# A second level of Strassen's algorithm in the second feed-forward matrix of an fp32 decoder block

## The chip, the cores and the metric

The kernel runs on one core of one Trainium2 chip. The metric is the device time of one execution in microseconds, from a median over several runs. Everything is computed in fp32.

## The reference

The input x has 4 batches of 2048 positions and 512 features. Three residual steps follow one another:

```
x = x + ssm(layernorm(x))              # linear recurrence over the 4 batches, features in groups of 64
x = x + cross_attention(layernorm(x))  # 16 heads of 32, 77 context rows for each batch
x = x + ffn(layernorm(x))

ffn: h = butterfly(x @ W_exp + b_exp, up_weights)      # 512 -> 2048, 11 butterfly stages
     h = gelu(h + up_bias)
     h = butterfly(h, down_weights)
     y = h @ W_con + b_con + down_bias                 # 2048 -> 512
```

The butterflies are linear, so the kernel multiplies them into the matrices beside them once: the feed-forward step becomes a 512 x 2048 matrix, a gelu, and a 2048 x 512 matrix. This case is about the second of the two.

## The kernel before

**Units.** The 2048 positions are cut into 16 units of 128. A unit has 4 x 128 rows (one tile of 128 for each batch), held as xt[P, 4, 512] with positions on the partitions. Each unit goes through `front` (recurrence, attention, the last layer norm and the sums `tb` that the first feed-forward matrix needs) and through `feed_forward`. The feed-forward of unit u and the front of unit u + 1 are woven together: `front` is a generator, and `step()` in `feed_forward` asks it for one more piece after every third step. A step is one product of the up half, or one of eight pieces of a product of the down half. A unit has 56 steps up and 56 down, and `front` has 33 pieces, so the front of the next unit ends before the unit does.

**Order on the engines.** The framework's scheduler orders each engine's instructions before the run, by the order of the code as priority and by its own estimate of when operands are ready; it adds all semaphores. An instruction whose operands are late in that estimate lets others go ahead, so matmuls of the two streams are mixed finely. SP issues all transfers, in one queue.

**One level of Strassen.** Both matrices use the seven-product form (Winograd's variant). For the second matrix (`down`, L606 to L643) the activations are four blocks a11, a12, a21, a22 of 1024 hidden rows by 256 positions, and the weights are seven combinations of 1024 x 256, made once in preparation and kept in DRAM as dn7 (L330 to L342). For each product `down` loads 1024 KB of weights into a buffer of the pool `wts` (three buffers, shared with the first matrix's w_up), and runs 8 x 2 matmuls: stationary an activation tile of 128 x 128, moving 256 columns of weights, summed over the eight hidden blocks in a PSUM bank:

```python
for p in range(h):
    for t in range(2):
        nc.tensor.matmul(ps[:, t, :], lhsT=act[p][lhs[i]][:, t, :], rhs=w[:, p, :], ...)
    step()
```

The products run in the order 5, 1, 6, 2, 7, 4, 3. Product 5 reads s1 = a21 + a22, which GpSimd makes for each hidden block in `up_tail` (L589). Between products GpSimd turns s1 into the other combinations (L621, L628), and VectorE adds the banks into xt, which is stored in four pieces.

**Attention, in `front`.** The query weights wq stay in SBUF for the whole run. For each batch tile: scores (L463), softmax on VectorE and ScalarE, scaling on GpSimd (L473), 16 transposes in four groups (L483) whose results pt are copied out of PSUM by VectorE and ScalarE in turn (L486, L488), the product with the values (L494) copied by VectorE into ot (L497), and the output projection (L501).

**Preparation.** `_prepare` builds both matrices before the first unit. The pieces of front(0) are woven in between. Its SBUF space (wup, wdn and smaller tiles) is given to the pools of the main loop (xlast, wts, ffn) afterwards, so these wait until its last stores have read it.

## Time and profile before

| | |
|---|---|
| median of 3 runs | 2728.4 us (2727.88 to 2728.4) |
| the profiled execution's own time | 2727.85 us |
| its span, first to last instruction | 2726.1 us |
| TensorE clock granted, mean | 0.990 |
| HBM read / written | 278.47 MB / 40.12 MB |
| w_dn loads | 112 of 1024 KB, 4.8 us to landing |
| w_up loads | 128 of 896 KB, 4.6 us to landing |

How to read it: PE is TensorE's matmuls, PEld its weight loads, which overlap the matmuls; DVE is VectorE, ACT ScalarE, POOL GpSimd, SP the engine that issues transfers. A group line gives line, engine, operation, output and inputs by the program's names, shapes and count, then busy us and the mean ns of one, then the engine's idle time just before and what ended it. An fp32 matmul stands in the profile as two records, each with its own weight load; a transpose is one record. [...]the rate is read from the starts of neighbours. The chain of waits is followed back from the last instruction to what released it each time.

### The profile page before, as it was taken

What the parts mean: (1) busy time and instruction counts of PE and PEld (TensorE: products, weight loads), DVE (VectorE), ACT (ScalarE), POOL (GpSimd) and SP (SyncE); (2) the same over time, 40 slices, a digit from 0 to 9 for tenths busy, and PEclk for the clock granted to TensorE, in tenths of its full rate; (3) what the DMA queues carried; (4) which work ended last, traced back from release to release, by engine and by line L of the source; (5) the groups of instructions that cost most, each with busy time, mean ns of one, the idle gap of its engine ahead of it and who ended that gap; (6) DMA issues with size and microseconds to landing.
All of it is one profiled execution on the core that took longest, in us unless ns stands there. A gap on an engine that the chain in (4) does not pass through costs nothing.

```text
span 2726.1 us, 34675 instructions
## 1 busy us (share of the span) xinstructions
PE 2626.3 (96%) x13448; PEld 2013.5 (74%) x13448; DVE 1308.1 (48%) x3148; ACT 794.3 (29%) x1456; POOL 778.7 (29%) x918
## 2 busy tenths in 40 slices
PE   6887999999999999999999999999999999999999
PEld 4545777786877778687777868777786877778688
DVE  4375544545454454545445454544545454454531
ACT  0222414223241422324142232414223241422321
POOL 4233231413223141322314132231413223141323
PEclk9888999999999999999999999999999999999999
DMA  7664233242423324242332424233232423323244
GB/s 234 213 246 173 89 111 110 78 135 78 143 89 112 111 76 135 78 143 89 113 109 77 135 78 143 89 114 109 76 136 78 143 89 111 112 77 120 78 141 137
DMA packets 96724, 320.84 MB, mean 118 GB/s; under 512 B 17584, under 2 KB 44336, under 8 KB 80432
## 3 DMA queue, kind: packets, MB, share of 16 engines
q1 hardware_dynamic: 96560, 318.62, 34.5%
q8 instruction: 107, 1.75, 0.2%
q14 instruction: 57, 0.47, 0.0%
HBM read 278.47 MB, written 40.12 MB: 117 GB/s over the span
## 4 chain that ended last, share of the span: by engine, by line
PE 83%; DVE 10%; POOL 4%; DMA 1%; issue 1%; ACT 0%; SPq 0%; POOLq 0%; DVEq 0%; ACTq 0%
PE ps_a L611 10%; PE ps_b L546 10%; PE ps_w L501 8%; PE ps_q L452 8%; PE ps_b L611 7%; PE ps_c L546 7%; PE ps_a L546 6%; PE ps_c L611 5%; PE ps_sc L463 5%; PE ps_pt L483 4%; PE ps_s L440 3%; POOL pr L473 2%; PE ps_t L399 2%; PE ps_o L494 2%; DVE st L377 2%
## 5 line engine op out<-in xcount | busy, mean ns | idle before, releaser
L589 POOL TENSOR_TENSOR s<-a,a 128x256 f32<-128x256 f32 x128 | 92.9, 726 | 1120.1 <-ACT a L551 1120.1
L546 PE MATMUL ps_b<-tb,w_up 128*128 128x256 f32 x1536 | 397.0, 379 | 0.7 <-DVE tb L518 0.7
L611 PE MATMUL ps_a<-w_dn,a 128*128 128x256 f32 x1536 | 372.1, 381 | 0.0
L611 PEld LDWEIGHTS ps_a<-w_dn,a 128*128 128x128 f32 x1536 | 282.3, 190 | 57.4 <-issue 20.3
L546 PEld LDWEIGHTS ps_b<-tb,w_up 128*128 128x128 f32 x1536 | 285.9, 190 | 51.1 <-issue 14.5
L551 ACT ACTIVATE a<-a,hbias 128x256 f32<-128x256 f32 x384 | 192.3, 508 | 270.4 <-DVE a L584 206.9
L546 PE MATMUL ps_a<-xnt,w_up 128*128 128x256 f32 x1024 | 269.0, 380 | 0.0
L611 PE MATMUL ps_c<-w_dn,s 128*128 128x256 f32 x1024 | 235.4, 381 | 7.3 <-POOL s L589 7.3
L501 PE MATMUL ps_w<-wo,ot 128*128 128x512 f32 x512 | 236.2, 604 | 4.8 <-DVE ot L497 4.8
L452 PE MATMUL ps_q<-xnt,wq 128*128 128x512 f32 x512 | 231.9, 596 | 0.7 <-ACT xnt L400 0.7
L611 PEld LDWEIGHTS ps_c<-w_dn,s 128*128 128x128 f32 x1024 | 191.0, 190 | 36.8 <-POOL s L589 11.4
L546 PEld LDWEIGHTS ps_a<-xnt,w_up 128*128 128x128 f32 x1024 | 190.4, 191 | 31.2 <-issue 7.2
L473 POOL TENSOR_TENSOR pr<-pr,sm 128x1232 f32<-128x1232 f32 x64 | 146.1, 2282 | 173.1 <-DVE sm L472 162.9
L501 PEld LDWEIGHTS ps_w<-wo,ot 128*128 128x128 f32 x512 | 96.3, 193 | 107.1 <-issue 94.4
L452 PEld LDWEIGHTS ps_q<-xnt,wq 128*128 128x128 f32 x512 | 97.9, 192 | 98.1 <-issue 93.9
L400 ACT COPY xnt<-ps_t 128x512 f32<-128x512 f32 x128 | 72.2, 588 | 331.4 <-PE ps_t L399 331.2
L469 ACT ACTIVATE pr<-pr 128x308 f32<-128x308 f32 x256 | 107.0, 455 | 206.7 <-DVE pr L468 206.2
L463 PE MATMUL ps_sc<-kbd,qt 128*128 128x308 f32 x512 | 163.3, 430 | 3.3 <-DVE pr L468 3.0
L483 PE MATMUL ps_pt<-ident,pr 128*77 128x128 f32 x1024 | 145.4, 281 | 19.2 <-POOL pr L473 13.6
L483 PEld LDWEIGHTS ps_pt<-ident,pr 128*77 128x77 f32 x1024 | 119.3, 150 | 56.5 <-POOL pr L473 19.7
L502 DVE TENSOR_TENSOR xt<-ps_w,xt 128x512 f32<-128x512 f32 x64 | 44.3, 692 | 235.0 <-PE ps_w L501 235.0
L599 POOL TENSOR_TENSOR xt<-xt,ybias 128x256 f32<-128x256 f32 x128 | 100.2, 818 | 184.4 <-DVE xn L396 184.4
(173 smaller groups left out, 3936.4 us busy)
## 6 DMA issues: line engine op xcount, KB each, us to landing
w_up<-up SPq DMA_DIRECT2D x128, 896.0 KB, 4.6
w_dn<-dn SPq DMA_DIRECT2D x112, 1024.0 KB, 4.8
xt<-in_x SPq DMA_DIRECT2D x16, 1024.0 KB, 5.5
out<-xt SPq DMA_DIRECT2D x64, 256.0 KB, 4.9
wdn<-in_wexp_t SPq DMA_DIRECT2D x4, 1024.0 KB, 10.9
rows_up<-wdn SPq DMA_DIRECT2D x16, 256.0 KB, 2.1
wdn<-rows_up SPq DMA_DIRECT2D x4, 1024.0 KB, 9.0
wdn<-in_wcon SPq DMA_DIRECT2D x4, 1024.0 KB, 4.8
```

The lines of the kernel that those rows point to most:

```text
L440: nc.tensor.matmul(ps[:, 2 * i : T, f * NS : (f + 1) * NS], lhsT=xpt[:, i, c * (P // NS) + f, :], rhs=gt[:, 0 : T - 2 * i, :], start=i == ...
L452: nc.tensor.matmul(ps, lhsT=wq[:, c, g * P : (g + 1) * P], rhs=xnt[:, c, :, :], start=c == 0, stop=c == NC - 1)
L463: nc.tensor.matmul(ps[:, 0 : 4 * NK], lhsT=qt[:, g, t, :], rhs=kbd[:, t, g, :], start=True, stop=True)
L469: nc.scalar.activation(pg, pg, AF.Exp, scale=1.0 / math.sqrt(DH))
L473: nc.gpsimd.tensor_tensor(pr, pr, sm.unsqueeze(2).to_broadcast([P, NH, NK]), ALU.mult)
L483: nc.tensor.transpose(pt_ps[0:NK, j, :], pr[:, 4 * g + j, :], ident)
L501: nc.tensor.matmul(ps, lhsT=ot[:, g, :], rhs=wo[:, g, :], start=g == 0, stop=g == NC - 1)
L546: nc.tensor.matmul(ps, lhsT=w[:, c, :], rhs=rhs[i - 1][:, c], start=first and c == 0, stop=c == 1, skip_group_check=True)
L551: nc.scalar.activation(out, x, AF.Gelu, bias=hbias[:, b : b + 1])
L589: nc.gpsimd.tensor_tensor(s1, a21, a22, ALU.add)
L599: nc.gpsimd.tensor_tensor(r, r, ybias[:, d], ALU.add)
L611: nc.tensor.matmul(ps[:, t, :], lhsT=act[p][lhs[i]][:, t, :], rhs=w[:, p, :], start=first and p == 0 and t == 0, stop=p == h - 1, skip_gro ...
```

## The change

The second matrix gets a second level: each of the seven products is itself done with seven products of 512 x 128 weights (49 in all).

- **Weights.** `_prepare` writes dn7[i] as seven 512 x 128 blocks: three copied as they are, four formed from the block by two VectorE and two GpSimd instructions in a double buffer. A product's weights are 1.75 MB and come in two loads of 1024 and 768 KB.
- **Activations.** The blocks a11 ... s1 become one tile each with eight hidden blocks, so that `operands` can form four combinations of four hidden blocks (512 columns) at a time, two on GpSimd and two on VectorE.
- **Matmuls.** 7 x 4 matmuls for each first-level product, with 128 moving columns; the seven results lie in two PSUM banks (tags a and b).
- **Folding.** One ScalarE copy and four VectorE sums take the seven results out of PSUM into pi, which is then added to the quarters of xt by VectorE or GpSimd.
- **Steps.** One step for each second-level product: 49 in the down half instead of 56. The order of first-level products becomes a11, s1, a12, s1 (changed), a22, s3, s1 (changed again). xt is stored in three pieces.
- **Attention.** wq no longer stays in SBUF; each unit loads it into the buffer of pt, which is now one tile for all four groups. All four pt copies and the ot copy are made by ScalarE.

```diff
@@ -27,6 +27,7 @@
 LOW = 7
 HIGH = 4
 LN_EPS = 1e-5
+DOWN = (0, 4, 1, 5, 3, 6, 2)
 MAGIC = 12582912.0
 
 
@@ -330,16 +331,23 @@
     h = NB // 2
     b11, b12, b21, b22 = (wdn[:, r * h : r * h + h, c * (D // 2) : (c + 1) * (D // 2)] for r in range(2) for c in range(2))
     t1, t2, t3, n4 = (wup[:, i, :].rearrange("p (b d) -> p b d", b=h) for i in range(4))
-    for i, w in ((0, b11), (1, b21), (2, b22)):
-        nc.sync.dma_start(out=dn7[i], in_=w)
     nc.vector.tensor_tensor(t1, b12, b11, ALU.subtract)
-    nc.sync.dma_start(out=dn7[4], in_=t1)
     nc.gpsimd.tensor_tensor(t3, b22, b12, ALU.subtract)
-    nc.sync.dma_start(out=dn7[6], in_=t3)
     nc.vector.tensor_tensor(t2, b22, t1, ALU.subtract)
-    nc.sync.dma_start(out=dn7[5], in_=t2)
     nc.vector.tensor_tensor(n4, b21, t2, ALU.subtract)
-    nc.sync.dma_start(out=dn7[3], in_=n4)
+    yield
+    st = pool.tile([P, 2, 4, h // 2, P], F32, tag="lowc", name="st")
+    y = (b11, b21, b22, n4, t1, t2, t3)
+    for n, i in enumerate(DOWN):
+        y11, y12, y21, y22 = (y[i][:, r * (h // 2) : (r + 1) * (h // 2), c * P : (c + 1) * P] for r in range(2) for c in range(2))
+        for k, w in ((0, y11), (1, y21), (6, y22)):
+            nc.sync.dma_start(out=dn7[i][:, k], in_=w)
+        s = st[:, n % 2]
+        nc.vector.tensor_tensor(s[:, 1], y12, y11, ALU.subtract)
+        nc.gpsimd.tensor_tensor(s[:, 3], y22, y12, ALU.subtract)
+        nc.vector.tensor_tensor(s[:, 2], y22, s[:, 1], ALU.subtract)
+        nc.gpsimd.tensor_tensor(s[:, 0], y21, s[:, 2], ALU.subtract)
+        nc.sync.dma_start(out=dn7[i][:, 2:6], in_=s)
     yield
 
 
@@ -358,7 +366,6 @@
     gt = const.tile([P, T, NS], F32, name="gt")
     kbd = const.tile([P, T, NC, 4 * NK], F32, name="kbd")
     vsb = const.tile([NK, T, D], F32, name="vsb")
-    wq = const.tile([P, NC, D], F32, name="wq")
     wo = const.tile([P, NC, D], F32, name="wo")
     hbias = const.tile([P, NB], F32, name="hbias")
     ybias = const.tile([P, D], F32, name="ybias")
@@ -443,6 +450,8 @@
             nc.vector.tensor_tensor(xc, ps, xc, ALU.add)
             yield
 
+        wq = work.tile([P, NC, D], F32, tag="pt", bufs=1, name="wq")
+        nc.sync.dma_start(out=wq, in_=wq_t.rearrange("(c p) e -> p c e", p=P))
         yield from normed(xt, got)
         xnt = got.pop()
         qt = work.tile([P, NC, T, P], F32, tag="qt", bufs=1, name="qt")
@@ -476,25 +485,20 @@
             if t == 0:
                 continue
             pr, tt = probs[t - 1], t - 1
-            pts = []
+            pt = work.tile([P, NC, 4, P], F32, tag="pt", bufs=1, name="pt")
             for g in range(NC):
                 pt_ps = psum.tile([P, 4, P], F32, tag="f", name="ps_pt")
                 for j in range(4):
                     nc.tensor.transpose(pt_ps[0:NK, j, :], pr[:, 4 * g + j, :], ident)
-                pt = work.tile([NK, 4, P], F32, tag="pt", bufs=4, name="pt")
-                if g % 2:
-                    nc.scalar.copy(pt, pt_ps[0:NK])
-                else:
-                    nc.vector.tensor_copy(pt, pt_ps[0:NK])
-                pts.append(pt)
+                nc.scalar.copy(pt[0:NK, g], pt_ps[0:NK])
             po = psum.tile([P, NC, P], F32, tag="f", name="ps_o")
             for g in range(NC):
                 for j in range(4):
                     h = 4 * g + j
                     nc.tensor.matmul(po[j * DH : (j + 1) * DH, g, :], lhsT=vsb[:, tt, h * DH : (h + 1) * DH],
-                                     rhs=pts[g][:, j, :], start=True, stop=True, tile_position=(0, j * DH))
+                                     rhs=pt[0:NK, g, j, :], start=True, stop=True, tile_position=(0, j * DH))
             ot = work.tile([P, NC, P], F32, tag="ot", bufs=1, name="ot")
-            nc.vector.tensor_copy(ot, po)
+            nc.scalar.copy(ot, po)
             yield
             ps = psum.tile([P, D], F32, tag="f", name="ps_w")
             for g in range(NC):
@@ -537,7 +542,7 @@
             return psum.tile([P, 512], F32, tag=tag, name=f"ps_{tag}")
 
         h = NB // 2
-        act = []
+        act = [ffn.tile([P, h, 2, P], F32, tag=g, bufs=1, name=g) for g in ("a11", "a12", "a21", "a22", "s1")]
         live = {}
 
         def up(p, i, ps, first):
@@ -567,19 +572,17 @@
         def up_mid(p):
             w, a, b, c, p1, u2 = live[p]
             up(p, 2, a, False)
-            a11, a12, a21, a22, s1 = (ffn.tile([P, 2, P], F32, tag=g, bufs=h, name=g)
-                                      for g in ("a11", "a12", "a21", "a22", "s1"))
+            a11, a12, a21, a22, s1 = (r[:, p] for r in act)
             gelu(a11, a, p)
             up(p, 7, b, False)
             u3 = ffn.tile([P, 2, P], F32, tag="u3", name="u3")
             nc.vector.tensor_tensor(u3, b, p1, ALU.add)
             nc.vector.tensor_tensor(a22, c, u3, ALU.add)
             gelu(a22, a22, h + p)
-            act.append((a11, a12, a21, a22, s1))
 
         def up_tail(p):
             w, a, b, c, p1, u2 = live[p]
-            a11, a12, a21, a22, s1 = act[p]
+            a11, a12, a21, a22, s1 = (r[:, p] for r in act)
             up(p, 4, b, False)
             nc.vector.tensor_tensor(a12, b, p1, ALU.add)
             gelu(a12, a12, h + p)
@@ -599,47 +602,74 @@
             nc.gpsimd.tensor_tensor(r, r, ybias[:, d], ALU.add)
         up_tail(h - 1)
-        a, b, c, b7, a4 = (bank(g).rearrange("p (t d) -> p t d", t=2) for g in "abcba")
-        lhs = {1: 0, 2: 1, 3: 4, 4: 3, 5: 4, 6: 4, 7: 2}
+        a11, a12, s3, a22, s1 = act
+        k = h // 2
         r11, r12, r21, r22 = (xt[:, t : t + 2, d : d + D // 2] for t in (0, 2) for d in (0, D // 2))
-        def down(i, ps, first):
-            w = wts.tile([P, h, D // 2], F32, tag="w", name="w_dn")
-            nc.sync.dma_start(out=w, in_=dn7[i - 1])
-            for p in range(h):
-                for t in range(2):
-                    nc.tensor.matmul(ps[:, t, :], lhsT=act[p][lhs[i]][:, t, :], rhs=w[:, p, :],
-                                     start=first and p == 0 and t == 0, stop=p == h - 1, skip_group_check=True)
+        def operands(x):
+            x11, x12, x21, x22 = (x[:, r * k : (r + 1) * k, t, :] for t in range(2) for r in range(2))
+            s1, s3, s2, s4 = (ffn.tile([P, k, P], F32, tag="sp", bufs=5, name="sp") for _ in range(4))
+            nc.gpsimd.tensor_tensor(s1, x21, x22, ALU.add)
+            nc.gpsimd.tensor_tensor(s3, x11, x21, ALU.subtract)
+            nc.vector.tensor_tensor(s2, x22, s3, ALU.subtract)
+            nc.vector.tensor_tensor(s4, x12, s2, ALU.subtract)
+            return (x11, x12, x22, s1, s2, s3, s4)
+        def down(i, x):
+            lhs = operands(x)
+            w = [wts.tile([P, n, k, P], F32, tag="w", name="w_dn") for n in (4, 3)]
+            nc.sync.dma_start(out=w[0], in_=dn7[i][:, 0:4])
+            nc.sync.dma_start(out=w[1], in_=dn7[i][:, 4:7])
+            ma, mb = (bank(g).rearrange("p (m q) -> p m q", m=4) for g in "ab")
+            for n, m in enumerate((ma[:, 0], ma[:, 1], mb[:, 1], mb[:, 2], ma[:, 2], mb[:, 0], mb[:, 3])):
+                for q in range(k):
+                    nc.tensor.matmul(m, lhsT=lhs[n][:, q, :], rhs=w[n // 4][:, n % 4, q, :], start=n in (0, 2) and q == 0,
+                                     stop=q == k - 1, skip_group_check=True)
                 step()
+            pi = ffn.tile([P, 2, 2, P], F32, tag="pi1" if i == 0 else "pi", bufs=1 if i == 0 else 2, name="pi")
+            u = ffn.tile([P, 2, P], F32, tag="u", bufs=1, name="u")
+            add = nc.vector.tensor_tensor
+            m1 = ffn.tile([P, P], F32, tag="m1", name="m1")
+            nc.scalar.copy(m1, ma[:, 0])
+            add(pi[:, 0], m1.unsqueeze(1).to_broadcast([P, 2, P]), ma[:, 1:3], ALU.add)
+            add(u, pi[:, 0, 1].unsqueeze(1).to_broadcast([P, 2, P]), mb[:, 0:3:2], ALU.add)
+            add(pi[:, 1], u[:, 0].unsqueeze(1).to_broadcast([P, 2, P]), mb[:, 1:3], ALU.add)
+            add(pi[:, 0, 1], u[:, 1], mb[:, 3], ALU.add)
+            return pi.rearrange("p t c q -> p t (c q)")
         def store(t, d, r):
-            nc.sync.dma_start(out=out[t : t + 2, u * P : (u + 1) * P, d : d + D // 2].rearrange("t p d -> p t d"), in_=r)
-
-        down(5, c, True)
-        nc.vector.tensor_tensor(r22, c, r22, ALU.add)
...
+            nc.sync.dma_start(out=out[t : t + 2, u * P : (u + 1) * P, d : d + r.shape[2]].rearrange("t p d -> p t d"), in_=r)
+        def both(engine, r, x):
+            x = x.unsqueeze(1).to_broadcast([P, 2, 2, D // 2])
+            engine.tensor_tensor(r, r, x, ALU.add)
+        right = xt[:, :, D // 2 : D].rearrange("p (h t) d -> p h t d", h=2)
+        lower = xt[:, 2:4, :].rearrange("p t (h d) -> p h t d", h=2)
+        p1 = down(0, a11)
+        nc.gpsimd.tensor_tensor(r11, r11, p1, ALU.add)
+        both(nc.vector, right, down(4, s1))
+        nc.vector.tensor_tensor(s1[:, 0:k], a22[:, 0:k], s3[:, 0:k], ALU.subtract)
+        nc.gpsimd.tensor_tensor(s1[:, k:h], a22[:, k:h], s3[:, k:h], ALU.subtract)
+        p2 = down(1, a12)
+        nc.gpsimd.tensor_tensor(r11, r11, p2, ALU.add)
         store(0, 0, r11)
...
-        store(2, 0, r21)
-        down(3, c, False)
-        nc.vector.tensor_tensor(r12, c, r12, ALU.add)
+        p6 = down(5, s1)
+        nc.vector.tensor_tensor(p6, p6, p1, ALU.add)
+        both(nc.vector, lower, p6)
+        nc.gpsimd.tensor_tensor(r12, r12, p6, ALU.add)
+        nc.vector.tensor_tensor(s1[:, 0:k], a12[:, 0:k], s1[:, 0:k], ALU.subtract)
+        nc.gpsimd.tensor_tensor(s1[:, k:h], a12[:, k:h], s1[:, k:h], ALU.subtract)
+        p4 = down(3, a22)
+        nc.gpsimd.tensor_tensor(r21, r21, p4, ALU.add)
+        both(nc.vector, lower, down(6, s3))
+        store(2, 0, xt[:, 2:4, :])
+        p3 = down(2, s1)
+        nc.vector.tensor_tensor(r12, r12, p3, ALU.add)
         store(0, D // 2, r12)
         for _ in other:
             pass
@@ -652,7 +682,7 @@
         return psum.tile([P, 512], F32, tag="abc"[turn[0]], name="ps_p")
 
     up7 = [dram.tile([P, 7, 2, P], F32, name=f"up7_{p}") for p in range(NB // 2)]
-    dn7 = [dram.tile([P, NB // 2, D // 2], F32, name=f"dn7_{i}") for i in range(7)]
+    dn7 = [dram.tile([P, 7, NB // 4, P], F32, name=f"dn7_{i}") for i in range(7)]
     xts = {0: load_x(0)}
     ready = []
     with tc.tile_pool(name="prep", bufs=1) as pool:
@@ -663,7 +693,6 @@
                         wup, wdn, hbias, up7, dn7)
         next(prep)
         _keys_values(nc, psum, ctx_t, wk_t, wv_t, kbd, vsb, wup)
-        nc.sync.dma_start(out=wq, in_=wq_t.rearrange("(c p) e -> p c e", p=P))
         nc.sync.dma_start(out=wo, in_=wo_t.rearrange("(c p) e -> p c e", p=P))
         db = wup[:, 3, 0:D]
         nc.sync.dma_start(out=ybias, in_=b_con.partition_broadcast(P))
```

## The prediction

> **What bounds the kernel now.** I read the page first (busy shares, then the shares of the chain of work that ended last), because they say whether one engine carries the time.
>
> ```profile
> PE 2626.3 (96%) x13448; PEld 2013.5 (74%) x13448; DVE 1308.1 (48%) x3148; ACT 794.3 (29%) x1456; POOL 778.7 (29%) x918
> PE 83%; DVE 10%; POOL 4%; DMA 1%; issue 1%; ACT 0%; SPq 0%; POOLq 0%; DVEq 0%; ACTq 0%
> ```
>
> TensorE is the bound: 96% busy and 83% of the chain. But a busy share can't say what another shape of matmul would cost, so the second view is TensorE's timeline at the end of one unit's second feed-forward matrix (start, length, engine, line).
>
> ```profile
> 1180.75 7.07 PE L611 MATMUL ps_a<-w_dn,a 128*128 128x256 f32 x32
> 1187.65 7.07 PE L611 MATMUL ps_c<-w_dn,s 128*128 128x256 f32 x32
> 1194.56 1.03 PE L546 MATMUL ps_a<-xnt,w_up 128*128 128x256 f32 x4
> ```
>
> 32 records from 1187.65 to 1194.56: one 256-column record each 0.2159 us with no gap. A logical fp32 matmul is two records (112 logical L611 matmuls a unit; the groups hold 3584 records for 16 units). The third view cuts a steady unit (it repeats each 159.0 us: up starts at 1035.6 and 1194.6) into its up half and its down half. The columns are length, then PE, PEld, DVE, ACT and POOL busy, clock, DMA share and GB/s.
>
> ```profile
> 1036.00:1111.60 75.60, 74.71 (x335) 59.03 (x334) 33.81 (x87) 30.25 (x57) 10.17 (x14) 1.00 0.34 119
> 1111.60:1194.60 83.00, 81.31 (x482) 61.95 (x481) 43.42 (x102) 18.22 (x33) 34.21 (x35) 1.00 0.28 96
> ```
>
> The change falls in the 83.0 us half: 224 x 0.2159 = 48.4 us of L611, some 33 us of the next unit's attention woven in, and under 2 us idle. VectorE is half busy there, GpSimd 41%.
>
> [...]in preparation, where 128-column matmuls (L284) run with a weight load each:
>
> ```profile
> 112.63 1.14 PE L284 MATMUL ps_p<-bd,wdn 128*128 128x128 f32 x8
> 113.60 0.28 PE L285 MATMUL ps_p<-b,bd 128*128 128x1 f32 x2
> 113.74 1.14 PE L284 MATMUL ps_p<-bd,wdn 128*128 128x128 f32 x8
> 114.86 1.14 PE L284 MATMUL ps_p<-bd,wdn 128*128 128x128 f32 x8
> ```
>
> Ten records, two of them one column wide, each 1.115 us: 0.1115 us a record even where the matmul is nothing. That is the weight load's pace. [...]at 256 columns the load hides, at 128 it is the pace. [...]L516 runs beside GpSimd's L517, L518 is the same shape mostly alone.
>
> ```profile
> L516 DVE TENSOR_TENSOR tb<-xnt 128x512 f32<-128x512 f32 x16 | 25.8, 1610 | 0.0
> L518 DVE TENSOR_TENSOR tb<-xnt,tb 128x512 f32<-128x512 f32 x16 | 10.9, 680 | 0.0
> L587 DVE TENSOR_TENSOR a<-ps_c,u 128x256 f32<-128x256 f32 x128 | 54.1, 423 | 43.1 <-PE ps_c L546 43.0
> L630 POOL TENSOR_TENSOR xt<-xt,u2d 128x512 f32<-128x512 f32 x48 | 59.7, 1272 | 0.0
> ```
>
> **The change part by part.**
>
> TensorE, each unit. Out: 112 logical matmuls, 224 records x 0.2159 = 48.4 us. In: 49 products x 4 = 196 logical matmuls of 128 columns, 392 records x 0.1115 = 43.7 us. Saved 4.6 us, times 16 = **-74 us**. Bounds of the pitch: 0.109 (transposes, eight in 0.87 us) gives -90; break-even is 48.4/392 = 0.1234, which no run of records in this trace reaches. I take 0.1115, since over 100 loads held it.
>
> Stalls that go. The start of the down half shows two waits (last column: idle before, releaser):
>
> ```profile
> 1115.74 1.10 PE L483 MATMUL ps_pt<-ident,pr 128*77 128x128 f32 x8 [0.91 <-POOL pr L473]
> 1122.52 1.13 PE L611 MATMUL ps_c<-w_dn,s 128*128 128x256 f32 x4 [0.49 <-POOL s L589]
> ```
>
> In the kernel before, product 5 comes first and needs s1 of all hidden blocks, the last made late on GpSimd, so TensorE runs out of filler. The new order starts with a11, which is complete earlier. At most 1.4 us a unit goes; next late is the pr multiplication (2.28 us on GpSimd) behind the new operand sums. I take -1.0 x 15 = **-15 us** (0 to -21).
>
> VectorE, down half of a unit. In: operand differences 14 x 0.68 = 9.5; folding seven products out of PSUM 7 x (3 x 0.423 + 0.29) = 10.9 (0.29 for 128 columns: between 0.423 at 256 and 0.692 at 512); sums into xt and s1 of 1024 elements 5 x 1.2 = 6.0 (between 0.68 at 512 and 2.29 at 2048, L335), two of 512, 1.4: 27.8. Out: seven sums of 0.69, eight pt copies of 0.677, four ot copies of 0.69: 13.0. So 43.4 becomes **58 us** of about 77. Of it 17 us have two SBUF inputs; at L516's stretch of 2.4 they take 41, and VectorE needs 82. GpSimd: in 18 x 1.27 + 2 x 2.3 (1024 elements, half of L337's 4.5) = 27.5, out 16 x 0.73 + 3 x 1.27 = 15.4: 34.2 becomes 46. ScalarE takes eight more pt copies, four ot copies and seven 128-column copies: 4.6 + 2.3 + 1.9 - 0.6 = +8 on 18; idle time hides it, and if exp queues behind it, softmax is late next. The operands are wanted a product (6.2 us or more) later and PSUM is double, so most of this hides; the softmax chain (max, subtract, sum on VectorE, the multiplication on GpSimd) shares the queues and has no such slack. I take 1.8 us of new TensorE stall a unit, x 15 = **+27 us** (0 to 6 us a unit: 0 to +90).
>
> Transfers. A product reads 1024 + 768 KB in two loads instead of 1024 KB in one; SP issues 14 weight loads instead of 7, one wq load more, one store fewer, 0.32 us each. The 1024 KB load lands in 4.8 us. With three buffers each load is issued a whole product ahead of need: 6.2 us bare, about 11 with attention woven in. Hidden for six products; in the seventh, and all through the last unit, only 1.4 us of slack is left. There VectorE and GpSimd also do a product's sums with no attention around: **+3 us** (0 to 8). wq goes through the pt buffer, free since the attention of the unit before, and is wanted some 10 us after it is traced: nothing, covered by up matmuls; uncovered it would cost its landing, about 5 us a unit. The last product's fold adds one copy and four sums ahead of the last store: **+2 us**.
>
> Preparation. Seven 1024 KB stores (dn7) become 21 of 256 KB and seven of 1024 KB, 12.3 MiB against 7, plus 28 sums of 512 elements (14 x 0.68 on VectorE, 14 x 1.27 on GpSimd, 27 us if they take turns). Before, the stores go out from 193 to 218 us, at 398 GB/s when dense:
>
> ```profile
> 208.00:213.00 5.00, 1.08 (x16) 0.60 (x16) 5.00 (x3) 0.00 (x0) 3.88 (x1) 0.64 1.06 398
> 213.00:218.00 5.00, 3.31 (x4) 1.51 (x5) 1.72 (x3) 0.00 (x0) 0.00 (x0) 0.50 0.95 393
> ```
>
> The first w_up loads follow at 218.8, into the space that preparation frees, and up starts at 237.95: some 14 us of slack after landing. The extra 5.5 MB need 14 us at that rate, [...]and the sums delay the first unit's attention, which waits for VectorE here already. **+10 us** (0 to 25).
>
> Sum: -74 - 15 + 27 + 3 + 2 + 10 = -47 on the profiled execution: span 2726.1, its own time 2727.85. That gives 2681; the median of the runs, 2728.4, lies 0.55 above. I say 2680 us.
>
> **Rivals.**
>
> *All of it hides* (0.20): no new stall, preparation +2: -74 - 21 + 4 = -91, 2637 us. For it: operands are wanted late, PSUM is double. Against: VectorE at 58 of 77 us leaves little room.
>
> *Weights late* (0.10): lateness of 2 us in each unit's seventh product adds 2 x 15 = 30: about 2710. For it: 1.4 us of slack and a store in the same queue. Against: today's seven 1024 KB loads a unit make TensorE wait nowhere.
>
> *VectorE and GpSimd become the bound, slower* (0.18): if the 17 us of two-input sums meet GpSimd each time, VectorE needs 82 us; with 3 us waiting for TensorE the down half is 85, against 83 now. +2 x 15 + 15 for preparation and the end = +45: 2773 us. It decides from the point where VectorE's down half passes 78. For it: L516; GpSimd busy 46 of 77. Against: overlap each time is the extreme.
>
> *The 128-column pace is worse* (0.05): beyond 0.1234 a record nothing is left, and preparation's and the end's 15 us remain: 2743. Against: the L284 stretch. That the change does not do what it says is not among these: the diff's loop counts give the 392 records.
>
> **How the numbers follow.** The forecast has 0.47. About 0.2% (5.5 us) is what a measurement of this kernel can tell from no change. Faster: 0.47 + 0.20 + 0.10 = 0.77; slower: 0.18 + 0.05 less 0.03 that falls within 0.2%: 0.20. The range goes from 2635 (full hiding) to 2745 (worse pace, and the near part of the VectorE rival); the far part and a still better pace are what is left out.
>
> **What would show it.** The down matmuls: 392 records a unit, 0.111 to 0.112 us apart where nothing else is woven in, weight loads busy nearly all of that time. A unit's period near 155 us instead of 159.0; the down half near 79. No wait for s (L589) at its start. VectorE 55 to 65 us busy in it, GpSimd about 46, differences of 512 elements at 0.68 to 1.6 us. TensorE's first up matmul at 240 to 255 us. Wrong if the period is 159 or more, if the pitch is above 0.12, or if w_dn loads release TensorE for more than 1 us a unit.

## The result and the profile after

| | before | changed |
|---|---|---|
| median | 2728.4 us | 2884.86 us (2876.57 to 2888.37) |
| ratio to before | 1 | 1.0569 [1.0547, 1.0592] |
| span of the profiled execution | 2726.1 us | 2882.4 us |
| a unit's period, mean of units 1 to 13 | 159.0 us | 167.9 us |
| TensorE clock granted, mean | 0.990 | 0.964 |

The change makes the kernel 5.7% slower; the forecast was 1.8% faster. The page of the changed kernel, busy shares and then the shares of the chain that ended last:

```profile
PE 2638.1 (92%) x16136; PEld 2118.2 (73%) x16136; DVE 1634.6 (57%) x3642; ACT 912.4 (32%) x1744; POOL 1065.4 (37%) x948
PE 57%; DVE 18%; POOL 13%; DMA 5%; ACT 4%; issue 2%; SPq 0%; POOLq 0%; ACTq 0%; DVEq 0%
```

TensorE's share of the chain fell from 83% to 57%. VectorE's, GpSimd's and the transfers' went from 15% to 36% together, although none of these engines is busy even 60% of the span. That is the picture of waits handed around, not of a new full engine. The steady unit, cut into up half and down half (length, then PE, PEld, DVE, ACT and POOL busy, clock, DMA share, GB/s):

```profile
1095.30:1176.70 81.40, 77.37 (x339) 60.51 (x338) 37.16 (x93) 30.48 (x57) 10.72 (x15) 0.98 0.37 125
1176.70:1262.60 85.90, 78.91 (x649) 66.58 (x648) 59.72 (x127) 25.34 (x51) 50.28 (x36) 0.98 0.47 155
```

The down half, forecast at 79, takes 85.9; the up half, which the change hardly touches, went from 75.6 to 81.4. VectorE is busy 59.7 us of the down half and GpSimd 50.3: near the amounts that the prediction worked out (58 and 46), with 26 us of VectorE's time idle. TensorE's timeline shows the pace and where the time is lost (start, length, instruction, idle before it and what ended it):

```profile
1093.49 1.95 PE L629 MATMUL ps_b<-w_dn,sp 128*128 128x128 f32 x16
1095.28 1.03 PE L551 MATMUL ps_a<-xnt,w_up 128*128 128x256 f32 x4
...
1103.58 1.68 PE L551 MATMUL ps_a<-xnt,w_up 128*128 128x256 f32 x4 [2.60 <-DMA w_up<-up]
...
1180.82 1.10 PE L492 MATMUL ps_pt<-ident,pr 128*77 128x128 f32 x8 [1.10 <-POOL pr L482]
...
1196.63 1.40 PE L472 MATMUL ps_sc<-kbd,qt 128*128 128x308 f32 x2 [3.24 <-DVE xt L506]
```

Sixteen records in 1.79 us are 0.112 us each: the pace is the one forecast. Most of the loss starts at two waits that the kernel before does not have in its units, 2.60 us for w_up in the up half and 3.24 us for the attention's sum L506 in the down half. TensorE's waits over the run (us in total, times, longest) have both once in nearly every unit:

```profile
PE ps_sc L472 <- DVE xt L506: 48.9, 16, 3.3
PE ps_a L551 <- DMA w_up<-up: 38.8, 15, 3.0
```

The same two groups of the kernel before have 0.3 us in the whole run for the sum (L502 there) and none for w_up:

```profile
L463 PE MATMUL ps_sc<-kbd,qt 128*128 128x308 f32 x512 | 163.3, 430 | 3.3 <-DVE pr L468 3.0 <-DVE xt L502 0.3
L546 PE MATMUL ps_a<-xnt,w_up 128*128 128x256 f32 x1024 | 269.0, 380 | 0.0
```

A smaller one grew with them: from unit 1 to unit 14 the transposes of the layer norm (L406) wait 30.9 us for VectorE, where the kernel before has 15.4.

**Where the 3.24 us come from.** VectorE's timeline before the wait:

```profile
1182.02 0.69 DVE L615 TENSOR_TENSOR sp<-a,sp 128x512 f32<-128x512 f32 x1 [2.64 <-POOL sp L614]
...
1183.36 1.43 DVE L480 TENSOR_REDUCE sm<-pr 128x16 f32<-128x1232 f32 x1
1184.82 0.25 DVE L481 RECIPROCAL sm<-sm 128x16 f32<-128x16 f32 x1
...
1191.44 1.74 DVE L615 TENSOR_TENSOR sp<-s,sp 128x512 f32<-128x512 f32 x1 [4.61 <-POOL sp L614]
1193.21 1.63 DVE L616 TENSOR_TENSOR sp<-s,sp 128x512 f32<-128x512 f32 x1
1194.77 1.21 DVE L656 TENSOR_TENSOR s<-a,a 128x1024 f32<-128x1024 f32 x1
1195.90 0.68 DVE L506 TENSOR_TENSOR xt<-ps_w,xt 128x512 f32<-128x512 f32 x1
```

and GpSimd's over the same stretch:

```profile
1178.51 2.25 POOL L482 TENSOR_TENSOR pr<-pr,sm 128x1232 f32<-128x1232 f32 x1
1180.72 1.27 POOL L614 TENSOR_TENSOR sp<-a 128x512 f32<-128x512 f32 x1
1185.22 2.25 POOL L482 TENSOR_TENSOR pr<-pr,sm 128x1232 f32<-128x1232 f32 x1 [3.23 <-DVE sm L481]
1187.43 0.72 POOL L592 TENSOR_TENSOR s<-a,a 128x256 f32<-128x256 f32 x1
1188.23 0.73 POOL L593 TENSOR_TENSOR a<-a,a 128x256 f32<-128x256 f32 x1
1188.91 1.26 POOL L613 TENSOR_TENSOR sp<-s 128x512 f32<-128x512 f32 x1
1190.13 1.27 POOL L614 TENSOR_TENSOR sp<-s 128x512 f32<-128x512 f32 x1
```

Read the two together. VectorE stands 2.64 us before L615, because GpSimd has the softmax multiplication L482 ahead of the sum L614. Meanwhile VectorE's own softmax sum L480 is stuck behind L615, so GpSimd then stands 3.23 us for L481. It catches up with L482, L592, L593, L613 and L614, and VectorE stands 4.61 us again. Each queue waits for the other in turn. L506, whose operand TensorE had ready at about 1192.4, is behind all that.

**Where the 2.60 us come from.** At the unit's end VectorE waits in the same way:

```profile
1089.99 1.74 DVE L615 TENSOR_TENSOR sp<-s,sp 128x512 f32<-128x512 f32 x1 [4.30 <-POOL sp L614]
...
1095.95 1.21 DVE L649 TENSOR_TENSOR xt<-xt,pi 128x1024 f32<-128x1024 f32 x1
```

L649 makes what the second output store (L644) sends, and that store is in SP's queue ahead of the next unit's weights:

```profile
1089.22 0.32 SPq L560 DMA_DIRECT2D w_up<-up  x1
1097.24 0.39 SPq L644 DMA_DIRECT2D out<-xt  x1
1097.74 1.28 SPq L560 DMA_DIRECT2D w_up<-up  x2
```

The first w_up load goes out at 1089.22, the second 8.5 us later, right behind the store (e1 below shows that it was the store that held it). The kernel before has its loads and stores in one queue too, but there the stores wait for late results for 0.8 us on average (6.5 at most). One of its four stores, then the changed kernel's second (us in total, times, longest):

```profile
SPq L616 <- DVE xt L632: 13.7, 16, 0.9
...
SPq L644 <- DVE xt L649: 121.8, 16, 7.8
```

**A third cost follows from these two.** The stretch after the 3.24 us wait (columns as in the table of halves):

```profile
1196.50:1200.00 3.50, 3.37 (x12) 2.93 (x13) 2.97 (x8) 1.95 (x3) 0.00 (x0) 0.57 0.00 0
```

The granted clock is 0.57 there. Between the starts of units 1 and 14 the trace has 25 stretches at 0.5, of 3.41 us each but for seven of twice that, 109 us in all: one after nearly each of the two waits. The kernel before has none in its steady part.

### The profile page after: what moved, and what is told of

Read it like the earlier page. It is cut to its first block, busy times and chain, and to the rows that moved or that the text cites. A ratio compares the mean times of both kernels' runs of the same rounds, so it can differ in the third digit from the quotient of the medians.

```text
span 2882.4 us, 41293 instructions
## 1 busy us (share of the span) xinstructions
PE 2638.1 (92%) x16136; PEld 2118.2 (73%) x16136; DVE 1634.6 (57%) x3642; ACT 912.4 (32%) x1744; POOL 1065.4 (37%) x948
## 4 chain that ended last, share of the span: by engine, by line
PE 57%; DVE 18%; POOL 13%; DMA 5%; ACT 4%; issue 2%; SPq 0%; POOLq 0%; ACTq 0%; DVEq 0%
PE ps_b L551 8%; PE ps_q L461 8%; PE ps_b L629 6%; PE ps_w L505 6%; PE ps_c L551 6%; PE ps_a L551 5%; PE ps_a L629 4%; POOL xt L602 3%; PE ps_sc L472 3%; DMA w_up<-up 3%; PE ps_s L447 3%; POOL sp L614 3%; DVE sp L615 3%; POOL pr L482 2%; PE ps_pt L492 2%
## 5 line engine op out<-in xcount | busy, mean ns | idle before, releaser
L592 POOL TENSOR_TENSOR s<-a,a 128x256 f32<-128x256 f32 x128 | 92.8, 725 | 1063.4 <-ACT a L556 823.4
L551 PE MATMUL ps_b<-tb,w_up 128*128 128x256 f32 x1536 | 408.1, 388 | 7.8 <-DVE u L568 7.8
L629 PE MATMUL ps_b<-w_dn,sp 128*128 128x128 f32 x2688 | 361.9, 279 | 0.0
L629 PEld LDWEIGHTS ps_b<-w_dn,sp 128*128 128x128 f32 x2688 | 332.9, 194 | 8.4 <-issue 6.2
L551 PE MATMUL ps_a<-xnt,w_up 128*128 128x256 f32 x1024 | 278.2, 391 | 38.8 <-DMA w_up<-up 38.8
L505 PE MATMUL ps_w<-wo,ot 128*128 128x512 f32 x512 | 230.6, 593 | 2.3 <-ACT ot L501 2.3
L472 PE MATMUL ps_sc<-kbd,qt 128*128 128x308 f32 x512 | 175.8, 456 | 51.7 <-DVE xt L506 48.9
L482 POOL TENSOR_TENSOR pr<-pr,sm 128x1232 f32<-128x1232 f32 x64 | 144.8, 2262 | 159.2 <-DVE sm L481 148.9
L493 ACT COPY pt<-ps_pt 77x512 f32<-77x512 f32 x256 | 137.8, 579 | 189.7 <-PE ps_pt L492 189.6
L492 PE MATMUL ps_pt<-ident,pr 128*77 128x128 f32 x1024 | 149.3, 285 | 37.8 <-POOL pr L482 22.2
L478 ACT ACTIVATE pr<-pr 128x308 f32<-128x308 f32 x256 | 105.0, 453 | 197.0 <-DVE pr L477 196.3
L505 PEld LDWEIGHTS ps_w<-wo,ot 128*128 128x128 f32 x512 | 92.5, 190 | 95.4 <-issue 92.3
L492 PEld LDWEIGHTS ps_pt<-ident,pr 128*77 128x77 f32 x1024 | 117.5, 151 | 59.9 <-POOL pr L482 25.9
L579 DVE TENSOR_TENSOR u<-ps_b,p 128x256 f32<-128x256 f32 x128 | 53.9, 421 | 189.3 <-PE ps_b L551 188.6
L472 PEld LDWEIGHTS ps_sc<-kbd,qt 128*128 128x128 f32 x512 | 94.4, 203 | 88.4 <-DVE xt L506 52.2
L615 DVE TENSOR_TENSOR sp<-s,sp 128x512 f32<-128x512 f32 x48 | 65.7, 1369 | 153.0 <-POOL sp L614 153.0
L587 DVE TENSOR_TENSOR a<-ps_b,p 128x256 f32<-128x256 f32 x128 | 54.0, 422 | 163.0 <-PE ps_b L551 163.0
```

What stands on the lines that cost most here:

```text
L472: nc.tensor.matmul(ps[:, 0 : 4 * NK], lhsT=qt[:, g, t, :], rhs=kbd[:, t, g, :], start=True, stop=True)
L478: nc.scalar.activation(pg, pg, AF.Exp, scale=1.0 / math.sqrt(DH))
L482: nc.gpsimd.tensor_tensor(pr, pr, sm.unsqueeze(2).to_broadcast([P, NH, NK]), ALU.mult)
L492: nc.tensor.transpose(pt_ps[0:NK, j, :], pr[:, 4 * g + j, :], ident)
L493: nc.scalar.copy(pt[0:NK, g], pt_ps[0:NK])
L505: nc.tensor.matmul(ps, lhsT=ot[:, g, :], rhs=wo[:, g, :], start=g == 0, stop=g == NC - 1)
```

## The experiments

Four ideas stood against each other. **Order**: what costs is what stands behind what in the engines' queues. **Amount**: VectorE and GpSimd have too much to do. **Volume**: 75% more weights through three buffers. **Copies**: ScalarE's additional ones. The expectations call them Q, L, V and S, and later "place in the queue" and "amount of work"; "chain" is the form of the first that was left in the end. "Period" below is the mean of units 1 to 13 of the profiled execution; the expectations name 167.4 or 167.5 for the changed kernel, where this mean is 167.9. Line numbers are the changed kernel's.

### Which part of the change costs the time

`e4`: the kernel before, with only wq loaded for each unit and all pt and ot copies on ScalarE.

> The kernel before with the attention part of the change alone: wq loaded by each unit into the pt buffer, all pt copies and the ot copy on ScalarE. Theories Q, L and V: no part of the loss, 2720 to 2740 us. Theory S (the four copies in a row on ScalarE hold up TensorE): 1 to 3 us a unit, 2745 us or more.

Measured: 2731.18 us, ratio 1.0008 [0.9998, 1.0019]. The attention's part costs nothing that can be told from zero; **copies** falls.

`e3`: the changed kernel without the four operand sums; the small products read x11, x12, x22, x21 instead.

```diff
-            nc.gpsimd.tensor_tensor(s1, x21, x22, ALU.add)
-            nc.gpsimd.tensor_tensor(s3, x11, x21, ALU.subtract)
-            nc.vector.tensor_tensor(s2, x22, s3, ALU.subtract)
-            nc.vector.tensor_tensor(s4, x12, s2, ALU.subtract)
-            return (x11, x12, x22, s1, s2, s3, s4)
+            return (x11, x12, x22, x21, x11, x12, x22)
```

> The changed kernel with the four operand sums of each product left out (plain blocks of the activations stand in their place; the 392 records and all transfers stay). Theories Q and L: most new waits go, period 153 to 157 us, 2690 to 2730 us with the longer preparation. Theory V: the w_up wait stays and the period is 163 us or more.

Measured: 2690.49 us in one run, period 155.3, neither of the two waits left. The down half:

```profile
1110.80:1189.80 79.00, 76.84 (x649) 65.42 (x648) 49.81 (x115) 25.41 (x51) 30.94 (x22) 1.00 0.52 174
```

Matmuls, folding and the streamed weights do what the prediction said. That 79.0 us is also the figure forecast is in part luck, since the forecast had counted the sums in. The 28 sums of 512 elements a unit, 14 on each engine, cost with all that they hold up the 12.6 us between 155.3 and 167.9.

`e1`: the changed kernel without the second of the three stores.

```diff
-        store(2, 0, xt[:, 2:4, :])
```

> The changed kernel without the store of xt's lower half between the sixth and the seventh product (half of the output stays unwritten). Theory Q (order in the queues): SP holds this store until VectorE's sum L649 is done and keeps the second w_up load behind it; without it the load goes out some 5 us earlier, TensorE's wait for DMA w_up (38.8 us in all, 2.6 us a unit) and the half-clock window after it go: a unit's period falls from 167.5 to about 163 us, 2815 us in all. Theory V (volume): two loads a product through three buffers are too slow in themselves; the wait stays and the period stays within 1 us of 167.5.

Measured: 2807.77 us in one run; the w_up wait is gone, the up half is 76.9 and the period 162.6. The scores' wait stays (49.2 us in 16 waits). The weights' volume and buffers are the same, so **volume** falls: w_up is late because of the store before it. This edit takes the store's bytes away as well; k1 below keeps them, and the wait goes there too.

### Is it enough to take the sums away from GpSimd?

`e2`: both GpSimd sums on VectorE.

```diff
-            nc.gpsimd.tensor_tensor(s1, x21, x22, ALU.add)
-            nc.gpsimd.tensor_tensor(s3, x11, x21, ALU.subtract)
+            nc.vector.tensor_tensor(s1, x21, x22, ALU.add)
+            nc.vector.tensor_tensor(s3, x11, x21, ALU.subtract)
```

> The changed kernel with all four operand sums of a product on VectorE (L613 and L614 moved from GpSimd). Theory Q: VectorE no longer stands 4 to 5 us behind a GpSimd sum with the xt sum of the attention (L506) queued after it; TensorE's wait for L506 (3.3 us a unit) goes, L649 and so the store come earlier and the w_up wait goes too: period 158 to 162 us, about 2780 us. Theory L (load: VectorE and GpSimd have too much to do): VectorE's down half grows from 60 to 69 us of 86, and the time is no better than 2870 us.

Measured: 2789.35 us, ratio 1.0216 [1.0199, 1.0233], period 162.0. That is close to what theory order forecast (158 to 162), but not by its mechanism: VectorE no longer stands for a GpSimd operand sum, and yet both of TensorE's waits stay (w_up with 29.5 us in 16), the scores' split in two:

```profile
PE ps_sc L472 <- DVE xt L506: 50.3, 29, 2.0
```

The down half shows why; VectorE is now busy 76.6 of 83.8 us:

```profile
1148.00:1231.80 83.80, 77.97 (x650) 65.34 (x648) 76.58 (x143) 28.48 (x53) 34.63 (x22) 1.00 0.48 159
```

Here **amount** is right in kind, though the time is far from its 2870: this version trades the waits between the queues for a queue that is nearly full.

### Taking away what the late sums hold up

`f1` gives ps_w a bank of its own, `g1` moves the stores to ScalarE's queue as well, `g2` adds a third buffer for the preparation's st, `g3` adds e2's edit.

```diff
-            ps = psum.tile([P, D], F32, tag="f", name="ps_w")
+            ps = psum.tile([P, D], F32, tag="c", name="ps_w")
...
-            nc.sync.dma_start(out=out[t : t + 2, u * P : (u + 1) * P, d : d + r.shape[2]].rearrange("t p d -> p t d"), in_=r)
+            nc.scalar.dma_start(out=out[t : t + 2, u * P : (u + 1) * P, d : d + r.shape[2]].rearrange("t p d -> p t d"), in_=r)
```

> The changed kernel, and only the PSUM bank of the attention's output projection ps_w moved from the two banks that the scores share (f) to bank c, which the down half leaves free. The scores of the next tile then no longer wait for the sum L506, which stands behind the operand sums on VectorE. Theory Q (what costs time is the order in the in-order queues): the 3.2 us wait of the scores and the half clock after it go, 4 to 5 us a unit; the w_up wait at the unit's end stays. Period 167.4 to about 163, time about 2815 us. Rival L (VectorE and GpSimd together have too much to do in the down half): the same sums are as late as before, so another wait on VectorE (scores to probabilities, or the norms) takes its place, and the period stays at 166 to 168, time 2865 to 2890.

> The same, and the three output stores of a unit issued from ScalarE's queue instead of SP's, so that the second w_up load of the next unit no longer stands behind the store that waits for the sum L649. Theory Q: both waits gone; the up half falls from 81.4 to about 77, the period to 157 to 159, time 2730 to 2755 us. Rival L: ScalarE's copies and exponentials now stand behind the waiting stores, or the late sums hold the next unit's first products by the tb and u sums; the period stays above 162, time over 2800.

> The same as the one before it, and three buffers instead of two for the preparation's tile st, so that VectorE's sums of the down matrix (L346) don't wait for the transfer to the DRAM copy. Theory 'the preparation waits for a buffer': the waits of 6.2 us go, the first up product comes 10 to 15 us earlier than 272.8, time 10 to 15 us under the kernel before it. Rival 'the preparation is bound by the bytes stored': the transfers take the same time one after another, the first up product moves by under 3 us, and so does the time.

> The same, and the operand sums L613 and L614 on VectorE instead of GpSimd, so that VectorE never waits for GpSimd inside an operand set. With the bank and the stores no longer holding TensorE, theory Q gives 1 to 2 us a unit less (period 156 to 157) since the rest of the late sums goes with the waits between the two engines. Theory L gives a period 1 to 4 us longer than without this edit, because VectorE at 76 us busy in a down half of 84 then sets the pace.

| | median, us | ratio to before | period |
|---|---|---|---|
| f1 | 2863.85 | 1.0492 [1.0458, 1.0525] | 166.1 |
| g1 | 2802.26 | 1.0280 [1.0254, 1.0306] | 163.0 |
| g2 | 2816.26 | 1.0320 [1.0302, 1.0337] | 163.3 |
| g3 | 2761.28 | 1.0125 [1.0110, 1.0140] | 160.4 |

f1 is a miss: I had read the bank as the cause, and of the 4 to 5 us expected 1.7 came. TensorE's wait is still there under another name, as the rival had it:

```profile
PE ps_sc L472 <- DVE pr L477: 49.5, 20, 3.1
```

L477 is a later VectorE instruction in the same late queue: here a bank between the late queue and its reader only renamed the wait (48.9 us in 16 waits for L506 in the changed kernel, 49.5 in 20 for L477 in f1). g1 takes the w_up wait away, as expected (up half 77.8), but the scores' wait stays, and 163.0 is a miss for theory **order**, which had 157 to 159 here; the rival's numbers (over 162, over 2800) held. g2 gained nothing, a miss too. g3 came to 160.4 where theory **order** had 156 to 157: with all four sums on VectorE its down half takes 84.2 us, VectorE busy 73 of them.

### Issuing the sums one product ahead

`h1` issues the two GpSimd sums of the next product after the fourth small product of the present one, and its two VectorE sums after the seventh. `h2` adds the stores on ScalarE's queue, `h5` one more thing: L614 (s3) on VectorE, L613 (s1) still on GpSimd.

```diff
-            lhs = operands(x)
+            lhs = ahead.pop()
...
+                if n == 3 and nxt is not None:
+                    o = operands(nxt)
+                    next(o)
+            if nxt is not None:
+                ahead.append(next(o))
```

> The changed kernel, and only the place of the operand sums in program order: the two GpSimd sums of the next product are issued after the fourth small product of the present one, and its two VectorE sums after the seventh, ahead of the sums that take the present product's result. The number of instructions stays. Theory 'place in the queue': VectorE no longer stands for 2 to 4 us before a GpSimd sum, so the attention's sums behind it come in time; the period falls from 167.4 to 159 to 162, with what stays due to the longer VectorE work itself; time 2760 to 2810. Theory 'amount of work' (VectorE and GpSimd slow each other down, and VectorE has no slack for what the attention needs at once): the period stays within 2 us of 167.4, time over 2850.

> The same, and the output stores issued from ScalarE's queue instead of SP's. If the w_up wait at the unit's end is still there after the edit before, this takes it away: the up half at 76 to 78 us, the period 1 to 4 us shorter than with the edit before alone. If the wait has gone with the edit before, the two agree within 10 us.

> The same, and the sum L614 (x11 - x21) on VectorE, L613 still on GpSimd. Under 'place in the queue' it changes little (under 1 us a unit), since the sums come ahead of their use anyway. Under 'amount of work' VectorE's 0.69 to 1.7 us for each of seven sums more makes the attention later: 1 to 4 us a unit longer; or, if it is GpSimd beside VectorE that stretches VectorE's two-input sums, 1 to 3 us a unit shorter, as the step from the ScalarE stores to all sums on VectorE was (163.5 to 160.4).

Measured: h1 2888.12 us, 1.0590 [1.0574, 1.0605], period 168.0; h2 2820.57, 1.0344 [1.0327, 1.0361], 163.7; h5 2722.01, 0.9981 [0.9972, 0.9990], 157.3. h1 changed nothing, which is the number of theory amount, but VectorE's timeline says why (L618 is the sum that was L615, L615 the one that was L614):

```profile
1194.12 1.74 DVE L618 TENSOR_TENSOR sp<-s,sp 128x512 f32<-128x512 f32 x1 [4.81 <-POOL sp L615]
```

The scheduler orders the queues by its own estimate of readiness and put the sums nearly where they had been; the wait is the same. So h1 is no test of what an earlier place would bring. The jump is between h2 and h5: one sum moved, 6.4 us a unit, more than twice what the most hopeful of h5's expectations had.

### The moved sum and the stores' queue, each alone and both

```diff
-            nc.gpsimd.tensor_tensor(s3, x11, x21, ALU.subtract)
+            nc.vector.tensor_tensor(s3, x11, x21, ALU.subtract)
```

`j1` is this edit alone, `j2` has g1's stores with it, `j3` h1's order. `k1` is the changed kernel with the edit of the stores only.

> The changed kernel, and only L614 (s3 = x11 - x21) on VectorE instead of GpSimd. In a set only s1 = x21 + x22 is then GpSimd's, and no VectorE sum reads it. Theory 'chain across the two queues' (VectorE stands for L614, meanwhile GpSimd runs out of work because its next softmax multiplication waits for VectorE): VectorE's 229 us of waits for GpSimd's sp go, the 3.2 us wait of the scores goes, the period falls from 167.4 to 158 to 161; time 2740 to 2790. Rival 'amount of work': seven sums more on the busier engine, the period 163 or more as when both sums went to VectorE (162), time over 2790. Rival 'only the place in program order helps': over 2790 too, with the scores' wait still 2 us or more.

> The same, and the stores issued from ScalarE's queue. Theory 'chain': what stays of the w_up wait at the unit's end goes, period 157 to 158.5, time 2718 to 2740. If the place in program order matters beside it, this stays 2 us a unit or more above 157.3, the period of the version that has all three edits: over 2750.

> The sum L614 on VectorE and the sums issued one product ahead, stores on SP as in the changed kernel. Theory 'chain': within 2 us a unit of j1, and the w_up wait decides what it loses against the version with all three edits (2722): 2725 to 2770. If the late sums were what made the store wait, there is no w_up wait here, and the time is within 10 us of 2722.

> The changed kernel, and only the output stores issued from ScalarE's queue. If the two causes are independent, it takes away what the same edit took away beside the moved sum: 3.5 us a unit (160.4 to 156.9), so the period is 163.5 to 164.5 with the scores' wait of 3.2 us still there, time 2820 to 2840. If the w_up wait has its root in the late sums alone, the period stays over 166.

| period (median, ratio to before) | stores in SP's queue | stores in ScalarE's queue |
|---|---|---|
| s3 on GpSimd | 167.9 (2884.86; 1.0569 [1.0547, 1.0592]) | k1 163.8 (2819.05; 1.0342 [1.0320, 1.0364]) |
| s3 on VectorE | j1 160.3 (2761.35; 1.0130 [1.0103, 1.0156]) | **j2 156.9 (2713.46; 0.9965 [0.9949, 0.9980])** |

The two edits are nearly independent: 4.1 and 7.5 us alone, 10.9 together. Two words in the source turn a loss of 5.7% into a gain of 0.35%. j3 (2762.31, 1.0138 [1.0122, 1.0154], period 160.3) equals j1: issuing the sums earlier in the program adds nothing. The halves of j1, then of j2:

```profile
1060.60:1140.90 80.30, 77.15 (x339) 60.61 (x338) 36.16 (x92) 30.45 (x57) 10.15 (x14) 0.98 0.37 127
1140.90:1221.10 80.20, 77.67 (x650) 65.44 (x649) 66.72 (x135) 28.34 (x53) 43.74 (x29) 1.00 0.49 166
```

```profile
1040.70:1117.40 76.70, 75.43 (x339) 59.33 (x338) 36.19 (x92) 30.43 (x58) 10.16 (x14) 1.00 0.37 128
1117.40:1197.50 80.10, 77.57 (x649) 65.34 (x648) 66.61 (x135) 28.06 (x52) 43.74 (x29) 1.00 0.50 172
```

The moved sum shortens the down half from 85.9 to 80, the stores' queue the up half from 80.3 to 76.7. In j2 the granted clock is 1.00 in both halves. Moving s3 puts 7 us more on VectorE and still wins, against **amount**: in a set of four sums, s3 is the only one of GpSimd's that a VectorE sum reads (s2 = x22 - s3). s1 is read by TensorE alone, so with s3 moved VectorE has nothing to stand for inside a set. Less contention between the two engines, which h5's expectation named, is not what won either: L615 and L616 do shorten (two sets in a row took 0.69, 0.69, 1.74 and 1.63 us at 1182 to 1195 in the changed kernel, and 0.68, 0.69, 0.69 and 0.89 at the same place in j2, 1122 to 1131), but VectorE's whole busy time rises from 96.8 to 102.8 us a unit. What goes is its waiting for L614, 13.9 us a unit. Moving s1 too gives 3.5 us a unit back (g3 against j2, which differ also in ps_w's bank and the third st buffer), and that part fits amount. At L506, j2's VectorE is early by 2.15 us:

```profile
1136.50 0.69 DVE L506 TENSOR_TENSOR xt<-ps_w,xt 128x512 f32<-128x512 f32 x1 [2.15 <-PE ps_w L505]
```

One thing stays open. With s3 on VectorE the scheduler also laid out TensorE's order otherwise: some ten more small matmuls now stand ahead of L505 and the scores, which are asked for later. How much of the 7.5 us is VectorE being early and how much TensorE asking later, these runs don't separate.

### The preparation

`p1` makes the second-level weight sums for two of the seven blocks only, with the same bytes stored. `j4` is h5, and `k2` is j2, each with three buffers for st and the plain stores L344 on ScalarE's queue.

```diff
-            nc.sync.dma_start(out=dn7[i][:, k], in_=w)
+            nc.scalar.dma_start(out=dn7[i][:, k], in_=w)
```

> The changed kernel with the second-level sums of the preparation made for the first two of the seven blocks only; the other five store what is in the two buffers, so the same bytes are stored. Theory 'the sums and their buffer waits lengthen the preparation': unit 1 starts 8 to 15 us earlier than 425.2, and the time falls by as much. Rival 'the stores set it' : the first up product moves by under 3 us.

> All three edits (sum on VectorE, ahead, stores on ScalarE), and in the preparation the 21 plain stores of the down matrix (L344) on ScalarE's queue, with three buffers for st. Theory 'the sums' stores stand behind plain ones': VectorE's 6 us wait goes, the first up product comes 5 to 12 us before 273.9, time 2708 to 2718. Rival 'VectorE and GpSimd make the preparation long': first up product within 3 us, time within 4 us of 2722.

> s3 on VectorE, output stores on ScalarE's queue, and in the preparation the 21 plain stores (L344) on ScalarE's queue with three buffers for st. Period 156.9 as without the last edit; from the first matmul of the down matrix's preparation (L327) to unit 1 some 223 us instead of 231; time 2703 to 2711 against 2713. If the preparation's gain was chance, 2711 to 2718.

In the changed kernel VectorE waits for a buffer of st, the first w_up loads go out at 257 instead of 219, and TensorE's first up matmul starts at 272.8 instead of 237.95:

```profile
223.83 0.69 DVE L346 TENSOR_TENSOR st<-wdn 128x512 f32<-128x512 f32 x1 [6.21 <-DMA dn<-st]
```

Profiled executions reach the down matrix at times that differ by up to 8 us, so I count from the first matmul of L327 to the start of unit 1. That is 214.0 us before, 240.7 changed, 229.6 in e3, 227.0 in p1 (2877.03 us in one run), 231.0 in g1 and 236.3 in g2, 232.3 in h5 and 224.5 in j4, 230.8 in j2 and 223.0 in k2. The third buffer alone gains nothing (g2), and the buffer with its own queue for the plain stores takes 8 us off, twice. The sums carry a part: p1 has 13.6 us less than the changed kernel. But this figure holds unit 0 as well, and kernels whose preparation was not edited range from 229.6 (e3) to 241.2 (e1). Up to the first up product alone p1 takes 77.0 us, against 88.3 in the changed kernel and 82.1 to 88.9 in the others; its one time, 2877.03, lies among those of the changed kernel. j4: 2716.06 us, 0.9959 [0.9944, 0.9974]. k2: **2705.76 us, 0.9914 [0.9899, 0.9928]**, the best of the versions that compute the whole result, 0.9% faster than the kernel before; period 157.0.

## Why the prediction was wrong

The forecast was -47 us; the spans differ by +156. A period of 159 us or more was one of its own signs of being wrong. Term by term:

- **TensorE's pace, -74: right.** Between the starts of units 1 and 14 the sum of record pitches (for each record, the distance that neighbours of its shape keep where nothing waits) fell by 60.2 us in 13 units, 4.63 a unit against the 4.6 forecast.
- **Stalls that go, -15: didn't come.** The wait on s at the down half's start went as forecast, but pr at L492 is waited for 1.10 us and sp 0.19 us instead of 0.91 and 0.49 us. What would be late next was named, and given too little.
- **New stalls, +27: this is the step that failed.** 1.8 us a unit was taken and 6 was the end of its range. TensorE's time beyond that pace rose from 73.7 to 249.1 us in 13 units, +13.5 a unit; over 15 units that is +202. Of the 13.5 the two waits are 5.9 (42.1 and 34.1 us in 13 units), the longer ones at L406 1.2, and the half clock at most 4.2 (an estimate: half of its 109 us); the rest lies in smaller waits and was not followed up. The sentence at fault is "The operands are wanted a product (6.2 us or more) later and PSUM is double, so most of this hides". It asks whether TensorE gets its operands in time, which it nearly does (it waits 0.2 us a unit for sp, L615). It doesn't ask what stands behind a VectorE sum that waits for GpSimd. Behind it were L480, which GpSimd waits for, L506, which TensorE waits for, and L649, which the store on SP waits for, which w_up waits for. The softmax chain was named as having no slack, and then got no price of its own.
- **Busy time was right and beside the point.** What was ready did not go ahead of what waited: VectorE stood idle until 1182.02 for L614, although L480, behind L615, had had its last input from ScalarE's L478 at 1180.03; and L506 stood ready for some 3.5 us behind L615, L616 and L656. In such a queue the sum to make is of waits passed on.
- **Weights late, +3, and the tail, +2.** The last unit grew by 8.7 us (100.7 to 109.4) in spite of 4.6 us less pace in its down half. Of it 4.5 is the w_up wait with its slow stretch in the up half, where the weights of the other matrix are late, and 1.3 is the tail. The down half grew by 2.9: TensorE waits 2.95 us there for L615, with a stretch of 6.83 us at half clock. w_dn releases it once in the whole run, in this unit, for 0.6 us. The rival "weights late" had "a store in the same queue" among its reasons, but priced the wrong load.
- **Preparation, +10: too low, within its range of 0 to 25.** e3, whose unit 0 runs at the forecast pace, has 229.6 - 214.0 = 15.6 us more from L327 to unit 1, plus the 4.6 us that unit 0 should save: +20.
- **wq and ScalarE's copies at nothing: right** (e4).

Together -74 + 202 + 13 (the last unit, 8.7 + 4.6) + 20 = +161, against +156 in the spans.

The slower rival, "VectorE and GpSimd become the bound", had the right engines and the wrong mechanism. It decides once VectorE's down half passes 78 us; that was 59.7. The stretch it counts on is there, but not each time. This group holds three of the seven sums L615 of a unit; over all seven the mean is 1.04 us:

```profile
L615 DVE TENSOR_TENSOR sp<-s,sp 128x512 f32<-128x512 f32 x48 | 65.7, 1369 | 153.0 <-POOL sp L614 153.0
```

Means of 1369 ns for a 680 ns sum, and 153 us of waiting for 65.7 us of work. With the chain between the queues and the store out of the way, the sums cost j2 1.6 us a unit over e3, which leaves them out, and j2's period of 156.9 is 1.7 above the 155.2 that the forecast's terms give (159.0 - 4.6 - 1.0 + 1.8). The forecast was near for a kernel that didn't have these two faults.

## What to carry to other kernels

When a change puts a short producer on one engine and its consumer on another, list what stands behind the waiting consumer in its queue and who waits for that; busy shares don't show it. Keep a dependent chain on one engine, and give the other engine the sums that only TensorE reads (j1: 7.5 us a unit). Keep a store that waits for late results out of the queue that issues the next weights (k1: 4.1 us a unit).

## What the runs showed of the hardware that I had not expected

- **A wait of 2 to 3 us cost more than itself.** After its two waits TensorE's granted clock was 0.5 for 3.41 us, sometimes for twice that, in 25 stretches in 13 units of the changed kernel. From 1192.71 to 1196.12, most of it waiting for L506, it was 1.00, from 1196.12 to 1199.53 it was 0.50, and two records of L472 took 1.40 us there, against 0.68 at 1192.27. k1 and j1, which have one wait a unit left, have 0.98 in the half where it lies and 1.00 in the other. In the changed kernel all 25 stretches begin on one grid of 3.413 us (those at 1103.96 and 1196.12 are 27 times that apart). Each follows a grid interval in which TensorE stood idle for 2.03 us or more; the other intervals at full clock between units 1 and 14 had less than 1.8 us (1.77 at 431.53, the rest 1.50 or less), and no stretch follows them. If TensorE loses half of the 109 us, that is 55 us or some 4 us a unit, an estimate of the most it can be.
- **Another queue for a store was worth more than its issue time.** Three stores take 0.39 us each to issue, but k1 gained 4.1 us a unit, 3.6 of it in the up half (81.4 to 77.8). In the changed kernel the w_up load behind the waiting store L644 went out at 1097.74, 8.5 us after the load before it.
- **A 0.69 us VectorE sum beside a GpSimd multiplication took longer than that multiplication.** In j2, s3 took 2.52 us (L615, of the same shape, 0.68 at 1122.33) where L482 on GpSimd took 2.25, and ended 0.54 us after it:

```profile
1119.22 2.25 POOL L482 TENSOR_TENSOR pr<-pr,sm 128x1232 f32<-128x1232 f32 x1
1119.49 2.52 DVE L614 TENSOR_TENSOR sp<-a 128x512 f32<-128x512 f32 x1
```

The next pair met the other way round: s3 began at 1125.64 and took 0.63 us, and L482, from 1125.87, took 2.50.
